# Latent attention: value products capped at four key tiles a step, a pair's last block in the step of tile 3, queries projected in two other steps

## The chip, the cores and the metric

The kernel runs on one core of a Trainium2 chip. The metric is the device time of one execution in microseconds (us). Three timed runs of the kernel before gave a median of 2326.03 us, with a lowest of 2324.08 and a highest of 2330.73. Engines are named as in the profile: PE is TensorE, DVE is VectorE, ACT is ScalarE, POOL is GpSimd, and SP is the engine whose queue issues most DMAs here.

## The reference

The computation has four layers over an input x of shape (2, 1024, 128), all in float32. Each layer is a normalization, an attention and a residual add, then a normalization, a feed-forward block and a residual add. The four attentions are called a, b, c and d after their tiles. Layer a shares one key and value head among 16 query heads and has no mask. Layer b is ordinary causal attention. Layer c is causal attention over a latent of 32 columns. Layer d is causal with biases. After a and b stands a quantized dense layer, after c and d a mixture of experts. The change touches layer c only:

```python
q_blhd = jnp.einsum('bld,dhk->blhk', x_bld, Wq)
latent_bll = jnp.einsum('bld,dc->blc', x_bld, Wkv_down)
k_blhd = jnp.einsum('blc,chk->blhk', latent_bll, Wk_up)
v_blhd = jnp.einsum('blc,chk->blhk', latent_bll, Wv_up)
attn = jnp.einsum('bqhd,bkhd->bhqk', q_blhd, k_blhd) / jnp.sqrt(jnp.asarray(HD, dtype=x_bld.dtype))
attn = jax.nn.softmax(jnp.where(mask, attn, neg_inf), axis=-1)
y_blhd = jnp.einsum('bhqk,bkhd->bqhd', attn, v_blhd)
return jnp.einsum('bqhd,hdo->bqo', y_blhd, Wout)
```

In the kernel the two up-projections are absorbed into the query weight and the output weight (`absorb`), so scores and value products of layer c work on the 32 latent columns themselves.

## The kernel before

**Units and steps.** A unit is one pair of heads of one batch of one layer: 4 layers x 2 batches x 8 pairs = 64 units, in that order. A unit of a causal layer has five steps, numbered i = 0 to 4, and a step takes the query tiles (128 rows each) listed in

```python
CAUSAL_STEPS = [[7], [6, 0], [5, 1], [4, 2], [3]]
```

so steps 0 to 3 each hold eight key tiles of scores for each head and step 4, that of tile 3, holds four. One loop runs over all steps of all units. The order is written out by hand (`tc.manual_schedule()`): every engine executes its instructions in the order in which this loop issues them.

**What one step issues, in this order.** (1) `transposes` of the step two places back: PE transposes probabilities (tiles `pp`, L788) and ACT copies them, or, for query blocks 2 and 3, DVE transposes them in 32 x 32 blocks into `slots` (L771). When a block of 256 query rows is complete, `blocks_moved` issues 16 DMAs on SP that reorder it into `prT` (L746). In front of this, `normalize` of the step one place back runs: DVE forms the reciprocal (L697) and POOL multiplies the probabilities (L701). (2) `add_products`: POOL adds finished outputs to x (L889). (3) `scores`: PE products `sc` (L634) and masks (L649), then DVE maxima `nmax` (L678). (4) `exponentials` on ACT (L689). The two score tiles in PSUM, one for each head, are reused by the next step, so its products wait for these exponentials. (5) `out_product` of what was finished in the step before: PE `po` (L866), and an ACT copy (L873). (6) `project`: a part of the next unit's projections, as many as the list `when` says for this step; in layer c a part is one half of the queries, one PE product of 128 x 512 in two passes (`pq`, L532) and one ACT copy (L540). (7) A part of the side work (normalizations and feed-forward blocks of the other batch). (8) `weigh_some`: value products `av` (L840) from a queue. (9) In step 4 the projection stands here, behind (8).

**The queue of value products.** The 1024 query rows of a unit are four blocks of 256 rows. They are accumulated in one PSUM tile, in the order of `BANKS`: block 3, then blocks 0 and 1 together, then block 2. A part of the queue is one key tile of one block. Block 3 has 8 parts, block 0 has 2, block 1 has 4 and block 2 has 6: 20 parts a unit. Block 3 and block 0 enter the queue in step 0 of the next unit, block 1 in step 1, block 2 in step 2. Blocks 2 and 3 come through the DMAs and enter two steps after their last transposes. The last part of a bank brings an ACT copy (L856), and the next step issues its `out_product`.

`weigh_some(4)` takes four parts and stops behind the last of a bank. If the end of a bank is among the next two parts, it goes on to that end. Counted out over steps 0 to 4, it issues 4, 4, 6, 6 and 0 parts: all of bank [0, 1] in step 2, all of block 2 in step 3, none in step 4.

**Around the layer.** The query weight of layer c is loaded by one DMA (`wq_c`, L1096) at the start of the last unit of layer b, behind the 16 DMAs of a block on SP. The projections of the first unit of layer c are issued in that same unit.

Of the kernel before, what the change touches and what calls it, by code (L numbers as in the profile page):

```python
# [36 lines left out]
def kernel(ctx: ExitStack, tc: tile.TileContext, a: dict, out: bass.AP):  # L37
# [30 lines left out]
    def load_attn(names):  # L68
        w = {}
        for key, src in names.items():  # L70
            ap = a[src]
            if key == "wo":
                t = wpool.tile([P, NPAIR, D], F32, tag="wo", name=f"wo_{src}")
                nc.sync.dma_start(out=t, in_=ap.rearrange("(c p) d -> p c d", p=P))
            elif key == "wk2":
                t = wpool.tile([D, 2, DH], F32, tag=key, name=f"{key}_{src}")
                for h in range(2):
                    nc.sync.dma_start(out=t[:, h, :], in_=ap)
            else:
                t = wpool.tile(list(ap.shape), F32, tag=key, name=f"{key}_{src}")  # L80
                nc.sync.dma_start(out=t, in_=ap)
            w[key] = t
        return w
# [177 lines left out]
    def moe_group(nm, b, g, last, xT, eng=nc.gpsimd, other=None):  # L261
# [139 lines left out]
    layers = [  # L401
        dict(nm="a", causal=False, kind="shared", ffn=dense_group, fnm="f"),
        dict(nm="b", causal=True, kind="full", ffn=dense_group, fnm="g"),
        dict(nm="c", causal=True, kind="latent", ffn=moe_group, fnm="m"),
        dict(nm="d", causal=True, kind="bias", ffn=moe_group, fnm="n"),
    ]
# [191 lines left out]
    def blocked(u, qb):  # L598

        if qb not in BLOCKED[layers[u[0]]["kind"]]:  # L600
            return 0
        nk = keys(u, qb * TPA + TPA - 1)
        return nk if layers[u[0]]["causal"] else nk - 1
# [4 lines left out]
    def step_of(u, qts):  # L608
        k = f"{tag_of(u)}_{qts[0]}"
        at = {}  # L610
        if len(qts) == 2:
            at = {qts[1]: 0, qts[0]: keys(u, qts[1]) * P}
        else:
            at = {qts[0]: QB - min(QB, keys(u, qts[0]) * P // 2)}
        pr = probp.tile([P, 2, S], F32, tag="pr", name=f"pr_{k}")
        tot = small.tile([P, 2, len(qts)], F32, tag="tot", name=f"tot_{k}")
        return dict(u=u, qts=qts, at=at, k=k, pr=pr, tot=tot)
# [66 lines left out]
    def exponentials(st, h, sc, nmax):  # L684

        u, tot = st["u"], st["tot"]
        for n, qt in enumerate(st["qts"]):
            c = slice(st["at"][qt], st["at"][qt] + keys(u, qt) * P)
            nc.scalar.activation(  # L689
                st["pr"][:, h, c], sc[:, c], AF.Exp, bias=nmax[:, n : n + 1],  # L690
                accum_out=tot[:, h, n : n + 1],
            )

    def normalize(st):
        u, pr = st["u"], st["pr"]
        rec = small.tile([P, 2, len(st["qts"])], F32, tag="rec", name=f"rec_{st['k']}")
        nc.vector.reciprocal(out=rec, in_=st["tot"])  # L697
        for h in range(2):
            for n, qt in enumerate(st["qts"]):
                c = slice(st["at"][qt], st["at"][qt] + keys(u, qt) * P)  # L700
                nc.gpsimd.tensor_scalar(  # L701
                    out=pr[:, h, c], in0=pr[:, h, c], scalar1=rec[:, h, n : n + 1], scalar2=1.0,
                    op0=ALU.mult, op1=ALU.mult,
                )
# [176 lines left out]
    def add_products():  # L881


        apply_coefficients()
        while adds:
            add_one(*adds.popleft())
# [47 lines left out]
    def some(queue, n):  # L934

        while n >= 1 and queue:
            try:
                next(queue[0])
                n -= 1
            except StopIteration:  # L940
                queue.popleft()
        return n
# [3 lines left out]
    def side_part():  # L946


        while side:
            try:  # L950
                said[0] = next(side[0])
                return
            except StopIteration:
                side.popleft()
        said[0] = None

    side, products, outs, waiting, complete, done = deque(), deque(), deque(), deque(), {}, {}
# [3 lines left out]
    def begin(u):  # L961
        for bank in banks(u):
            for qb in bank:
                late.append(dict(key=(u, qb), bank=bank, ready=None))

    def release():

        x = late.popleft()
        (u, qb), bank = x["key"], x["bank"]
        assert x["ready"] is not None  # L970
        nkt = keys(u, (qb + 1) * TPA - 1)
        products.extend(
            (u, qb, bank, kt, qb == bank[-1] and kt == nkt - 1) for kt in range(nkt)
        )

    def weigh_some(n):

        while n and products:
            part = products.popleft()
            weigh(*part)  # L980
            n -= 1
            if part[-1]:
                return
        if any(x[-1] for x in [*products][:2]):
            while not part[-1]:
                part = products.popleft()
                weigh(*part)
# [97 lines left out]
    for step, (n, u, qts, i, total) in enumerate([*steps, *[(None, None, None, 0, 1)] * 4]):  # L1085
        new = None
        if n is not None:
            if n != last:
                last = n
                some(coming, 9)  # L1090
                if n + 1 < len(units):
                    nu = units[n + 1]
                    if nu[:2] != u[:2]:
                        if nu[0] == 2 and 2 not in weights:
                            wq = wpool.tile([D, H * DH], F32, tag="wq", name="wq_c")
                            nc.sync.dma_start(out=wq, in_=c_wqk.rearrange("d p h c -> d (p h c)"))  # L1096
                            weights[2] = {"wq": wq}
                        elif nu[0] not in weights:
                            weights[nu[0]] = load_attn(w_names[nu[0]])
                        while nu[:2] not in xTs:  # L1100
                            side_part()
                    coming.append(project(nu))


                    if layers[nu[0]]["kind"] == "shared":
                        when = [0, 0, 1, 0, 1, 0, 0, 0]
                    elif layers[nu[0]]["kind"] == "latent":
                        when = [1, 1, 0, 0, 0]
                    elif total == NT:
                        when = [0, 1, 1, 0, 1, 1, 1, 1]  # L1110
                    else:
                        when = [1, 1, 2, 0, 2]
            new = step_of(u, qts)


        st = waiting.popleft() if len(waiting) == 2 or not new and waiting else None
        if st:
            if st["u"] not in begun:
                begun.add(st["u"])
                begin(st["u"])  # L1120
            for _ in transposes(st):
                if last_step:
                    normalize(last_step.pop())
            for qb in {qt // TPA for qt in st["qts"]}:
                if complete[st["u"], qb] == TPA:
                    x = next(x for x in late if x["key"] == (st["u"], qb))
                    x["ready"] = step + (2 if blocked(st["u"], qb) else 0)
        if last_step:
            normalize(last_step.pop())
        add_products()  # L1130
        if new and said[0] == "early":
            side_part()
            share -= 1
        if new:
            sc, nmaxs = scores(new)
            for h in range(2):
                exponentials(new, h, sc[h], nmaxs[h])
            last_step.append(new)
            waiting.append(new)
        while copies:  # L1140
            nc.scalar.copy(*copies.popleft())
        while outs:
            out_product(*outs.popleft())

        values = new and i >= (total - 2 if total == NT else total - 1)
        if new and coming and not values:
            some(coming, when[i])
        share = min(share + (1.8 if n is None else SIDE[u[0]]), 3.0)
        while share >= 1 and side:
            side_part()  # L1150
            share -= 1
            if said[0]:
                break


        while late and late[0]["ready"] is not None and late[0]["ready"] <= step:
            release()
        weigh_some(4)
        if values and coming:
            some(coming, when[i])  # L1160
    while products or late or outs or side:
# [67 lines left out]
```

## Time and profile before

| | value |
|---|---|
| median of the timed runs | 2326.03 us |
| profiled execution | 2320.46 us, of which the span from first to last instruction is 2318.7 us |
| mean granted clock of PE | 0.968 |
| busy share of the span | PE 91%, DVE 74%, ACT 63%, POOL 55% |
| scores of layer c on PE (`sc_c`) | from 1192.5 to 1678.2 us |
| first and last start of its value products (`av_c`) | 1226.6 and 1703.8 us |
| parts of projections of layer c (`pq_c`) | 32, in 64 passes, from 1167.1 to 1627.7 us |

The busy shares are means over stages that differ. Layers a, b and d keep PE almost without a gap. In layer c the products are short and PE waits more. The place of the layer is read from the first and last start of its tiles. The clock column is the share of full speed that PE was granted: where it says 0.50, a product takes about twice as long.

### The profile page before, as it was taken

To read this page: it belongs to the slowest core of one execution; us is meant where nothing else is said; L and a number is where in the kernel's file an instruction comes from. 1 tells how busy PE (TensorE), PEld (TensorE's weight loads), DVE (VectorE), ACT (ScalarE), POOL (GpSimd) and SP (SyncE) were. 2 spreads that over 40 slices of the span, in tenths; PEclk is the share of its full clock that TensorE was granted. 3 is DMA by queue.
4 is the path that set the end of the run, shared out by engine and by line. 5 is a ranking of instruction groups with operands and counts; after the bars stand their busy time and mean duration, and the time that the engine had idled before them with its cause. 6 is when DMAs were issued, how large, how long until landed. Compare 5 with 4: busy or idle time off the path is not lost.

```text
span 2318.7 us, 43436 instructions
## 1 busy us (share of the span) xinstructions
PE 2111.9 (91%) x14833; PEld 1234.0 (53%) x14833; DVE 1717.2 (74%) x2695; ACT 1450.9 (63%) x3276; POOL 1282.9 (55%) x1723
## 2 busy tenths in 40 slices
PE   6999999999999999999987888888889999999986
PEld 2454444444445666666654444444455666656653
DVE  5979999999986876678668867867666656766544
ACT  3667676667765666666655566665666557666552
POOL 3756666767764554464545645655554446544441
PEclk8999999999999999999998889999899999999997
DMA  5767676667776666666655555554665446646450
GB/s 126 164 150 168 162 165 162 146 144 165 167 195 147 160 155 158 163 157 154 147 122 132 128 128 128 136 120 101 159 160 137 118 115 158 159 118 146 109 135 9
DMA packets 147195, 328.84 MB, mean 142 GB/s; under 512 B 48800, under 2 KB 59296, under 8 KB 146976
## 3 DMA queue, kind: packets, MB, share of 16 engines
q1 hardware_dynamic: 146976, 326.06, 59.5%
q8 instruction: 120, 1.97, 0.4%
q14 instruction: 99, 0.81, 0.1%
HBM read 10.27 MB, written 2.10 MB: 5 GB/s over the span
## 4 chain that ended last, share of the span: by engine, by line
PE 53%; DVE 13%; SPq 13%; ACT 8%; DMA 6%; issue 4%; POOL 2%; DVEq 0%; ACTq 0%; POOLq 0%
SPq L746 13%; PE av_a L845 6%; PE sc_a L634 6%; PE av_d L845 5%; DMA prT<-slots 5%; PE sc_d L634 4%; DVE slots L771 4%; PE sc_b L634 4%; PE av_b L845 3%; ACT pr_c L689 3%; PE sc_c L634 2%; DVE nmax_d L678 2%; DVE nmax_a L678 2%; DVE nmax_c L678 2%; PE pp_d L788 2%
## 5 line engine op out<-in xcount | busy, mean ns | idle before, releaser
L689 ACT ACTIVATE pr_a<-sc_a,nmax_a 128x1024 f32<-128x1024 f32 x256 | 282.8, 1109 | 216.0 <-DVE nmax_a L678 215.2
L701 POOL TENSOR_SCALAR pr_a<-pr_a,rec_a 128x1024 f32<-128x1024 f32 x256 | 283.4, 1118 | 188.2 <-DVE rec_a L697 187.8
L701 POOL TENSOR_SCALAR pr_d<-pr_d,rec_d 128x1024 f32<-128x1024 f32 (+7 forms) x256 | 186.3, 745 | 269.0 <-DVE rec_d L697 268.7
L678 DVE TENSOR_REDUCE nmax_a<-sc_a 128x1 f32<-128x1024 f32 x256 | 298.8, 1206 | 35.9 <-PE sc_a L634 35.4
L701 POOL TENSOR_SCALAR pr_b<-pr_b,rec_b 128x1024 f32<-128x1024 f32 (+7 forms) x256 | 186.8, 747 | 219.9 <-DVE rec_b L697 219.4
L701 POOL TENSOR_SCALAR pr_c<-pr_c,rec_c 128x1024 f32<-128x1024 f32 (+7 forms) x256 | 186.9, 747 | 207.0 <-DVE rec_c L697 207.0
L678 DVE TENSOR_REDUCE nmax_d<-sc_d 128x1 f32<-128x1024 f32 (+7 forms) x256 | 177.2, 748 | 149.8 <-PE sc_d L640 149.8
L689 ACT ACTIVATE pr_c<-sc_c,nmax_c 128x1024 f32<-128x1024 f32 (+7 forms) x256 | 186.3, 738 | 152.3 <-DVE nmax_c L678 125.4
L771 DVE STREAM_TRANSPOSE slots<-pr_a 128x896 f32<-128x896 f32 x256 | 279.0, 1094 | 3.0 <-DMA prT<-slots 1.5
L689 ACT ACTIVATE pr_b<-sc_b,nmax_b 128x1024 f32<-128x1024 f32 (+7 forms) x256 | 186.3, 738 | 146.6 <-DVE nmax_b L678 121.9
L634 PE MATMUL sc_a<-k_a,q_a 64*128 64x512 f32 x512 | 265.7, 633 | 11.7 <-ACT pr_a L689 11.5
L689 ACT ACTIVATE pr_d<-sc_d,nmax_d 128x1024 f32<-128x1024 f32 (+7 forms) x256 | 186.4, 738 | 135.2 <-DVE nmax_d L678 131.8
L634 PE MATMUL sc_a<-k_a,qx_a 64*128 64x512 f32 x512 | 263.1, 635 | 4.1 <-DMA qx_a<-q_a 4.0
L678 DVE TENSOR_REDUCE nmax_b<-sc_b 128x1 f32<-128x1024 f32 (+7 forms) x256 | 176.7, 746 | 88.6 <-PE sc_b L640 88.6
L845 PE MATMUL av_a<-prT,v_a 128*64 128x256 f32 x1792 | 223.0, 388 | 18.3 <-DMA prT<-slots 17.5
L678 DVE TENSOR_REDUCE nmax_c<-sc_c 128x1 f32<-128x1024 f32 (+7 forms) x256 | 176.9, 748 | 84.5 <-PE sc_c L649 83.7
L845 PEld LDWEIGHTS av_a<-prT,v_a 128*64 128x64 f32 x1792 | 122.5, 137 | 133.5 <-issue 76.4
L634 PE MATMUL sc_d<-k_d,q_d 64*128 64x512 f32 (+3 forms) x416 | 159.9, 497 | 0.3 <-ACT pr_d L689 0.3
L634 PE MATMUL sc_b<-k_b,q_b 64*128 64x512 f32 (+3 forms) x416 | 158.9, 494 | 1.1 <-ACT pr_b L689 1.1
L634 PE MATMUL sc_d<-kx_d,qx_d 64*128 64x512 f32 (+3 forms) x416 | 154.2, 490 | 0.2
L634 PE MATMUL sc_b<-kx_b,qx_b 64*128 64x512 f32 (+3 forms) x416 | 153.4, 488 | 0.7 <-ACT pr_b L689 0.6
L771 DVE STREAM_TRANSPOSE slots<-pr_b 128x1024 f32<-128x1024 f32 (+3 forms) x128 | 130.5, 1025 | 9.4 <-DMA prT<-slots 8.6
(407 smaller groups left out, 4743.7 us busy)
## 6 DMA issues: line engine op xcount, KB each, us to landing
prT<-slots SPq DMA_DIRECT2D x768, 128.0 KB, 2.3
prT<-slots SPq DMA_DIRECT2D x832, 112.0 KB, 2.2
prT<-slots SPq DMA_DIRECT2D x768, 96.0 KB, 2.1
qx_a<-q_a SPq DMA_DIRECT2D x32, 256.0 KB, 3.5
qx_b<-q_b SPq DMA_DIRECT2D x32, 256.0 KB, 3.6
kx_b<-k_b SPq DMA_DIRECT2D x32, 256.0 KB, 3.4
qx_d<-q_d SPq DMA_DIRECT2D x32, 256.0 KB, 3.6
kx_d<-k_d SPq DMA_DIRECT2D x32, 256.0 KB, 3.5
```

Source lines behind the costliest of these rows:

```text
L634: yield nc.tensor.matmul(sc[h][:, at[qt] + k0 : at[qt] + k1], lhsT=q[r, qt * P : (qt + 1) * P], rhs=kk[r, k0:k1], start=True, stop=not dia ...
L678: nc.vector.tensor_reduce(out=nmax[:, n : n + 1], in_=sc[h][:, c], axis=AX.X, op=ALU.max, negate=True)
L689: nc.scalar.activation(st["pr"][:, h, c], sc[:, c], AF.Exp, bias=nmax[:, n : n + 1], accum_out=tot[:, h, n : n + 1],)
L701: nc.gpsimd.tensor_scalar(out=pr[:, h, c], in0=pr[:, h, c], scalar1=rec[:, h, n : n + 1], scalar2=1.0, op0=ALU.mult, op1=ALU.mult,)
L746: nc.sync.dma_start(out=o, in_=x)
L771: nc.vector.transpose(dst, src.rearrange("p (k r q) -> p k r q", r=4, q=32),)
L788: nc.tensor.transpose(pt[:, h, kt - k0, :], pr[:, h, c0 : c0 + P], ident)
L845: nc.tensor.matmul(shaped(av[ROWS[h], n], t0), lhsT=vs[u][:, kt, h, :], rhs=moving(h, kt, t0), start=(kt == 0), stop=(kt == nkt - 1),)
```

## The change

`weigh_some` gets a second argument, with which going on to the end of a bank is switched off. Where the head of the queue belongs to a latent unit, the loop asks for four parts a step, and for six in the last step of a unit. The list `when`, which places the two halves of a latent unit's queries, goes from steps 0 and 1 to steps 1 and 3.

```diff
-    def weigh_some(n):
+    def weigh_some(n, more=True):
...
-        if any(x[-1] for x in [*products][:2]):
+        if more and any(x[-1] for x in [*products][:2]):
             while not part[-1]:
                 part = products.popleft()
                 weigh(*part)
...
                     elif layers[nu[0]]["kind"] == "latent":
-                        when = [1, 1, 0, 0, 0]
+                        when = [0, 1, 0, 1, 0]
...
-        weigh_some(4)
+        if products and layers[products[0][0][0]]["kind"] == "latent":
+
+            weigh_some(6 if i == total - 1 else 4, False)
+        else:
+            weigh_some(4)
```

Counted out in the same way, the steps 0 to 4 now issue 4, 4, 4, 2 and 6 parts: two parts of bank [0, 1] go from step 2 to step 3, and all six of block 2 from step 3 to step 4. The out-products follow one step behind: that of bank [0, 1] goes from step 3 to step 4, that of block 2 from step 4 to step 0 of the next unit, and their additions to x on POOL go one step later too. No instruction is added or removed.

## The prediction

> **What bounds the kernel now.** The change lies between about 1160 and 1710 us, from the last unit of layer b to the first of layer d, so I read that stage alone. First the view of waits for PE there (who was waited for: total, times, longest):
>
> ```profile
> PE sc_c L634 <- ACT pr_c L689: 24.0, 47, 1.2
> PE pp_c L788 <- POOL pr_c L701: 19.1, 23, 2.7
> PE av_c L840 <- DMA prT<-slots: 9.3, 6, 2.2
> PE po_c L866 <- DMA wo_c<-c_wvo: 4.1, 1, 4.1
> PE pq_c L532 <- DMA wq_c<-c_wqk: 3.5, 1, 3.5
> ```
>
> PE waits here for three things that come back in every unit (exponentials before scores, POOL before the `pp` transposes, the DMA before value products) and for two that come once. Then the timeline of a unit without side work shows where they fall (start, duration, engine, line, tiles, count, gap and its releaser):
>
> ```profile
> 1427.72 0.70 PE L866 MATMUL po_c<-wo_c,attnT_c 128*128 128x128 f32 x4
> 1428.63 0.44 PE L788 MATMUL pp_c<-ident,pr_c 128*128 128x128 f32 x2 [0.21 <-POOL pr_c L701]
> 1429.96 0.66 PE L788 MATMUL pp_c<-ident,pr_c 128*128 128x128 f32 x4 [0.90 <-POOL pr_c L701]
> 1430.55 1.14 PE L634 MATMUL sc_c<-latT_c,q_c 32*128 32x512 f32 x8
> 1431.62 0.28 PE L649 MATMUL sc_c<-over_all,ident_b 128*128 128x128 bf16 x2
> 1431.74 1.08 PE L532 MATMUL pq_c<-xT,wq_c 128*128 128x512 f32 x2
> 1434.37 1.07 PE L840 MATMUL av_c<-prT,lat_c 128*32 128x256 f32 x16 [1.55 <-DMA prT<-slots]
> ```
>
> That is the end of step 4 and step 0 of the next unit. In step 4 PE has nothing between `po` and `pp`, and `pp` waits 1.1 us for POOL. In step 0 the products of block 3 wait for DMAs. Last, the view by windows of the same steps 3, 4 and 0, cut at the first score product (us, busy of each engine, granted PE clock):
>
> ```profile
> 1419.99:1425.67 5.68, 5.47 (x52) 3.07 (x52) 4.73 (x8) 3.86 (x12) 3.39 (x5) 1.00 0.32 74
> 1425.67:1430.55 4.88, 3.19 (x22) 1.85 (x21) 3.80 (x8) 4.29 (x13) 3.33 (x5) 1.00 0.92 208
> 1430.55:1436.40 5.85, 4.29 (x37) 2.04 (x37) 3.01 (x4) 3.86 (x8) 3.22 (x5) 1.00 0.79 183
> ```
>
> PE (first busy column) is busy 5.47 of 5.68 us in step 3, but 3.19 of 4.88 in step 4. Yet a step's floor is not PE's: it is the loop of scores, maxima, exponentials and the next scores, which the timeline gives as 5.6 us between the ends of exponentials in steps 1 to 3 of quiet units, and 3.2 in step 4. A second loop binds the unit: the block-3 transposes on DVE end in step 3 at 1422.48, 16 DMAs follow at 0.63 us each on SP, the products start at 1434.37 and the scores of step 1 at 1436.4. PE is the bound only in steps where its next scores start later than the exponentials allow. I call that lateness and read it for all 80 steps from their timelines (scores can start 0.14 us behind the first head's exponentials at best).
>
> **Part 1: the queries leave step 0; the border of b and c.** The first latent queries were issued in step 0 of b's last unit, in front of b's value products, and `wq_c` was just being loaded:
>
> ```profile
> 1163.36 0.24 PE L640 MATMUL sc_b<-over,unit 64*128 64x128 bf16 x2
> 1167.14 1.10 PE L532 MATMUL pq_c<-xT,wq_c 128*128 128x512 f32 x2 [3.54 <-DMA wq_c<-c_wqk]
> 1168.17 3.63 PE L845 MATMUL av_b<-prT,v_b 128*64 128x256 f32 x16
> 1171.73 1.09 PE L788 MATMUL pp_b<-ident,pr_b 128*128 128x128 f32 x8
> ```
>
> With the queries in steps 1 and 3 the b products come first. Their own 16 DMAs were issued by 1162.6 and the last landed at 1164.3, so they start there, after a wait of 0.7 us. In the next step the same 16 take 1.73 us, so they end at 1166.1; eight `pp` (their POOL input was done at 1161.7) end at 1167.1. Scores of step 1 then start near 1167.2 instead of 1172.75; the exponentials they need ended at 1166.2. That is 5.5 us earlier. `wq_c` lands at 1167.0, before the query product of step 1. The second query product (1.1 us) comes into step 3, but behind it stands step 0 of c's first unit, where b's products wait 2.9 us for DMAs that are set by an earlier transpose, so it is hidden. I take -5.3. The lower end is -2.4 (3.54 less 0.7, less 0.4 for a landing that is delayed): the clock behind the gap was half (3.63 us against 1.73), and may be half again.
>
> [...]
>
> ```profile
> 1386.70:1390.10 3.40, 2.54 (x17) 1.33 (x18) 2.44 (x4) 2.68 (x10) 1.16 (x2) 1.00 0.64 158
> 1390.10:1393.50 3.40, 3.40 (x33) 2.03 (x32) 3.40 (x5) 2.02 (x5) 1.53 (x3) 0.50 0.20 47
> ```
>
> PE was busy 2.54 of 3.40 us, its longest gap was 1.21, and the clock still fell to 0.50. By that row every thinned step can bring a half-speed stretch of 3.4 us, worth up to 1.7 us. But five such stretches begin behind a POOL wait in step 4 (1253.6, 1284.3, 1315.0, 1376.5, 1649.5), which the change fills. I take 0, with ends of -8 (five by 1.7) and +10 (six new ones).
>
> **Part 2: two parts leave step 2.** Six parts with two zero products took 1.49 us (1417.59 to 1419.08), and 24 passes without them 1.49; a part is four passes and 0.25 to 0.27 us. So step 2 loses 0.5 us. This counts where step 2 was late: by more than 0.5 in units 1, 2, 4, 5, 6, 10, 11, 13, 14 and 15, by 0.3 in unit 3, by nothing in 7, 8, 9 and 12. Unit 0 still works off b's queue.
>
> **Part 3: step 3.** It loses six parts (1.49) and the out-product of bank [0, 1] (1.11, row x8 at 1422.63), and gains two parts (0.5) and a query product (1.08): -1.0 us. It was late by that much only in units 4, 9, 10, 12, 13 and 14. On ACT the query copy (0.6) comes and the copy of the out-product (0.59) goes. The queue of SP and the DVE order are not touched in this step.
>
> **Part 4: step 4.** It gains six parts (1.49), and its out-product grows from two query tiles to four (0.70 to 1.11): +1.9 to 2.0 us in front of `pp`, and behind `pp` the scores of the next unit. The POOL wait covers 1.1 us in quiet units, 1.8 to 3.8 in units 1, 2, 3 and 14, about 0.3 to 0.9 in the others. So the scores of step 0 come 0.9 us later in quiet units. What is late next there is the DMA of step 0: its landing is set by step 3's transposes, PE's wait of 1.55 shrinks, and the scores of step 1 start as before. Without that cover (units 4 and 5) it costs 1.1 and 0.9, each less 0.45 from part 5. The ACT copy of block 2 (0.40) now queues in front of the `pp` copies and the exponentials of step 0; exponentials start at 1433.2 and these copies end near 1432.3: hidden. POOL loses an addition of 1.28 us here, behind which nothing urgent stood.
>
> **Part 5: step 0.** It loses a query product (1.08) and gains the out-product of block 2 (0.6): -0.45, worth something only where no DMA wait follows. The DMAs of block 2 (SP) write where the products of step 4 read, so they now wait for PE until about 1430.4 instead of 1425.2. But the DVE transposes in front of them end at 1431.0, and SP is busy with block 3 until 1432.6: nothing. Were SP held, 4.8 us without an issue lie before the next block's DMAs.
>
> **The sum.** Border -5.3. Unit 0: its step 3, late by 1.3, gains a query product, +1.0. Units 1 to 6: parts 2 and 3 give -3.8, parts 4 and 5 cost +1.1: -2.7. Units 7 to 9, bound by the DMA loop: 0. Units 10 to 13 carry the expert layer; there PE waits inside the side work for DVE, and what stands in front of that (`po`, `pq`) is hidden in every step, so only moved parts count: parts 2 and 3 give -4.5, part 4 costs 4 x 1.5 less some 3.0 of waits in step 4: -1.5. Unit 14: -1.3. Unit 15: its step 2 gives -0.5, its step 4 holds projections of d and has only 0.3 us of wait, +1.7, and as much as 0.3 of such waits falls due in d's first unit: +1.5. Together -8.3 us (border -5.3, +1.0, -2.7, -1.5, -1.3, +1.5). The side work of batch 0 also moves one step later, with the additions; its pieces keep their order and end in step 0 of unit 15, just in time; I count 0, with 3 us either way.
>
> The profiled span becomes 2318.7 - 8.3 = 2310.4 us (execution: 2312.2, with the same 1.8 around it). The median of the timed runs lies 5.6 above that execution; scaled, 2326.03 x 2310.4 / 2318.7 = **2317.7, so 2318 us**. Own range: 2311 to 2323, from the ends of the border and the noise of the side work.
>
> **Rivals.** (1) *Step 4 becomes the bound.* The pile-up of 2.0 us, less 1.1 of POOL wait, reaches the end in all 15 units and what steps 2 and 3 give up was covered by the exponentials: 15 x 0.9 = +13.5, border -5.3, together +8.2: 2334. For it: the exponentials are waited for 47 times. Against: the DMA wait of step 0. It decides once the distance from the scores of tile 3 to those of tile 7 grows by over 0.9 us while step 0 doesn't shrink. (2) *Only an exchange of waits.* The border's gain is taken back by the next DMA wait (2.9 us at c's first unit), the rest cancels: -1 to -3, so 2324. For it: quiet units are bound by the DMA loop. (3) *The clock gains.* A filled step 4 keeps full speed: another -8, so 2310.
>
> **How the numbers follow.** The forecast has 0.55, rival 1 0.22, rival 2 0.16, rival 3 0.07. About 0.3% (7 us) is what a measurement of this kernel can tell from no change. Faster by more than that, below 2319: rival 3 and two thirds of the forecast, 0.44. Within: the rest of the forecast and rival 2, 0.34. Slower: rival 1, 0.22. The range 2307 to 2332 leaves out about 0.1 at each end.
>
> **What would show it.** Right: no wait of `pq_c` for `wq_c`; scores at 1436.4 of the quiet unit unchanged against the start of its step 3; the `pp` wait for POOL well below 19.1 us. Wrong: quiet units longer than 26.3 us, more than 16% of the layer at half speed (mean clock 0.92), or `av_c` waiting on PSUM in step 4.

## The result and the profile after

The changed kernel takes 2333.01 us (median of 20 runs, 2324.92 to 2344.4), beside 2324.32 us for the kernel before (20 runs): a ratio of 1.0037, 95% interval [1.0025, 1.0049], or 8.7 us slower. The profiled execution took 2339.49 us (span 2337.8), in the upper part of those runs.

The view of waits for PE from 1160 to 1730 us, the changed kernel (who was waited for: total, times, longest):

```profile
PE sc_c L634 <- ACT pr_c L689: 30.0, 54, 1.7
PE cb_m L372 <- DVE sg_m L357: 10.5, 7, 1.7
PE pp_c L788 <- POOL pr_c L701: 9.3, 14, 1.2
PE av_c L840 <- DMA prT<-slots: 8.5, 6, 2.2
PE pp_c L788 <- ACT attnT_c L873: 2.3, 2, 1.4
PE gg_m L352 <- ACT q_c L540: 1.5, 1, 1.5
PE pt_d L174 <- POOL xn_d L157: 1.1, 1, 1.1
```

The wait for POOL halved (19.1 before) and that for `wq_c` (3.5) is gone, as foreseen. The wait for the exponentials grew from 24.0 to 30.0 us, and that of the second transposes for the copy of an out-product from 1.0 to 2.3. The wait of layer d's transposes for POOL is new. The expert layer's gate product now waits for the copy of the queries, 1.5 us; before, it waited 2.6 us for the copy of an out-product, so this wait is no loss.

The border of b and c in the timeline:

```profile
1163.44 1.95 PE L845 MATMUL av_b<-prT,v_b 128*64 128x256 f32 x16 [0.88 <-DMA prT<-slots]
1165.32 1.09 PE L788 MATMUL pp_b<-ident,pr_b 128*128 128x128 f32 x8
1166.35 0.59 PE L634 MATMUL sc_b<-k_b,q_b 64*128 64x384 f32 x1
...
1168.53 1.13 PE L532 MATMUL pq_c<-xT,wq_c 128*128 128x512 f32 x2
```

b's value products no longer stand behind the queries: they start 4.7 us earlier (1168.17 before), and the query product finds its weight there.

The quiet unit of the prediction, steps 4 and 0:

```profile
1419.83 2.08 PE L866 MATMUL po_c<-wo_c,attnT_c 128*128 128x128 f32 x8
1421.83 2.02 PE L840 MATMUL av_c<-prT,lat_c 128*32 128x256 f32 x24
1423.79 0.87 PE L788 MATMUL pp_c<-ident,pr_c 128*128 128x128 f32 x6
1424.59 1.14 PE L634 MATMUL sc_c<-latT_c,q_c 32*128 32x512 f32 x8
1425.66 0.28 PE L649 MATMUL sc_c<-over_all,ident_b 128*128 128x128 bf16 x2
1425.78 0.66 PE L866 MATMUL po_c<-wo_c,attnT_c 128*128 128x128 f32 x4
1427.52 1.07 PE L840 MATMUL av_c<-prT,lat_c 128*32 128x256 f32 x16 [1.08 <-DMA prT<-slots]
```

The same stretch by windows (us, busy of PE, PEld, DVE, ACT and POOL, granted clock, DMA share and rate): first step 3, then the end of step 3 with the beginning of 4, then the rest of step 4, then the whole of step 4 and step 0.

```profile
1411.89:1417.52 5.63, 4.64 (x30) 1.88 (x30) 4.68 (x8) 3.32 (x11) 3.39 (x5) 1.00 0.31 70
1416.00:1419.40 3.40, 1.99 (x14) 1.02 (x12) 2.54 (x5) 3.38 (x10) 1.15 (x3) 1.00 0.87 199
1419.50:1424.60 5.10, 5.10 (x44) 3.39 (x42) 3.26 (x6) 3.24 (x9) 4.58 (x7) 0.67 0.93 207
1417.52:1424.59 7.07, 6.43 (x49) 3.98 (x49) 4.38 (x8) 5.21 (x14) 4.95 (x7) 0.76 0.94 210
1424.59:1429.55 4.96, 3.88 (x39) 2.26 (x38) 2.36 (x2) 3.05 (x7) 0.35 (x1) 1.00 0.57 132
```

Step 4 takes 7.07 us (4.88 before), step 0 4.96 (5.85), step 3 5.63 (5.68): the three together are 1.3 us longer, not equal. Step 0 does give some back, for its DMA wait shrank as foreseen (1.55 to 1.08). But the pile-up in step 4 did not run at the price that I gave it. PE was busy only 1.99 of 3.40 us around the border of steps 3 and 4; then the clock fell, and `po` x8 with the six parts took 2.08 and 2.02 us where full speed gives 1.11 and 1.49, as in step 3 of the kernel before:

```profile
1422.63 1.11 PE L866 MATMUL po_c<-wo_c,attnT_c 128*128 128x128 f32 x8
1423.67 1.49 PE L840 MATMUL av_c<-prT,lat_c 128*32 128x256 f32 x24
```

The units in which the time went are read from the first exponential of each. A second profile of the kernel before was taken (span 2325.2); it has 174 us at half speed where the first has 147, and the last two columns compare the change with both. In this second one the three steps of the quiet unit take 16.95 us, against 16.41 in the first and 17.66 in the change.

| stretch | forecast | against the first profile | against the second |
|---|---|---|---|
| a and b up to the border | 0 | -1.0 | -1.3 |
| border of b and c | -5.3 | -4.5 | -4.4 |
| unit 0 | +1.0 | +0.8 | +0.5 |
| units 1 to 6 | -2.7 | -2.4 | -1.8 |
| units 7 to 9 | 0 | +3.6 | -1.0 |
| units 10 to 13 | -1.5 | **+9.7** | **+8.3** |
| units 14, 15 and d's first | +0.2 | **+8.2** | **+7.5** |
| the rest of d | 0 | +4.7 | +4.8 |
| sum | -8.3 | +19.1 | +12.6 |

The sums are those of single executions; the medians differ by 8.7. Most of the loss lies in units 10 to 15 of batch 1, where the expert layer runs beside the attention, and behind them.

### The profile page after: what moved, and what is told of

It reads as the page before. It is cut to its first block, busy times and chain, and to the rows that moved or that the text cites. A ratio compares the mean times of both kernels' runs of the same rounds, so it can differ in the third digit from the quotient of the medians.

```text
span 2337.8 us, 43429 instructions
## 1 busy us (share of the span) xinstructions
PE 2139.5 (92%) x14833; PEld 1244.7 (53%) x14833; DVE 1714.4 (73%) x2695; ACT 1453.2 (62%) x3276; POOL 1285.1 (55%) x1723
## 4 chain that ended last, share of the span: by engine, by line
PE 49%; SPq 16%; DVE 15%; ACT 8%; DMA 5%; issue 5%; POOL 3%; DVEq 0%; ACTq 0%; POOLq 0%
SPq L746 15%; PE sc_a L634 6%; PE av_a L845 5%; DMA prT<-slots 4%; DVE slots L771 4%; PE av_d L845 4%; PE sc_d L634 4%; PE sc_b L634 3%; PE av_b L845 3%; ACT pr_c L689 3%; PE sc_c L634 3%; DVE nmax_d L678 2%; DVE nmax_a L678 2%; DVE nmax_c L678 2%; PE av_c L840 2%
```

## The experiments

Times are medians; a ratio is to the kernel before, with its 95% interval. No kernel leaves work out; the filler products of some are read by nobody.

The expectations weigh the forecast's accounting against theories of the loss. *Pile-up*: the 2 us more in step 4 stand in front of the next unit's scores and no wait covers them. *Side work*: the normalizations and expert-layer pieces that follow a batch start once its last output has been added, and so one step later. *Clock*: steps with less work bring more stretches at half speed, such as the one behind the 1.99 busy us of 3.40 above. *PSUM* (from the runs within batch 1 on): out-products, query products and transposes take their PSUM tiles from one pool of three.

### The two halves of the change, and the side work

**Queries alone** (only the list `when` of the change).

> Kernel before with the list of the queries alone changed (steps 1 and 3 in place of 0 and 1). All three theories on the loss of the change leave this part out, so each expects the gain at the border of layers b and c alone: about 5 us less than before (ratio 0.998), no wait of pq_c for wq_c, and the rest of layer c as before. If it is not faster, moving the queries costs something that I have not seen, and the border's gain is taken back inside layer c.

Measured: 2325.86 us, 1.0020 [1.0011, 1.0028]: slower, although the border's gain is in it. Its waits show the price:

```profile
PE av_c L840 <- DMA prT<-slots: 19.9, 8, 3.6
```

That was 9.3 before. Without the query product PE reaches the value products of step 0 sooner and stands there, up to 3.6 us, before the DMAs have landed. No theory had foreseen this; all had expected 5 us less.

**Products alone** (the change without its line `when`).

> The changed order of value products alone, queries in steps 0 and 1 as before. Measured for the whole change is +8.7 us (ratio 1.0037); with a border gain of 5 us taken out, every theory expects about +13 us here (ratio 1.0055). They differ in where: pile-up theory: in step 4 of units 9 to 15; side-work theory: from unit 9 on, in the steps that hold the large pieces of the expert layer, whichever these are; clock theory: wherever the half-speed stretches lie, with some 45 us more at half speed over the span, each us at half speed worth up to half a us.

Measured: 2347.3 us, 1.0111 [1.0093, 1.013], 25.7 us slower where every theory had expected 13, and far worse than the whole change. A wait that was 1.0 us before has grown:

```profile
PE pp_c L788 <- ACT attnT_c L873: 12.3, 12, 2.3
```

`po`, `pq` and `pp` all take their PSUM tile from one pool of three (`ps_m`). With block 2's out-product and a query product both in step 0, the second transposes find none free until ACT has copied the out-product: twelve waits. With the queries moved away, two are left (2.3 us). That is 10 of the 17 us between the two kernels at most; the rest is not explained.

**Side work late**: the kernel before, but the side work behind layer c's batches enters one step later, as the later additions make it do in the change.

```diff
-            side.append(between(li, b))
+            (shifted if li == 2 else side).append(between(li, b))
```

> Kernel before, with value products and queries as they were; only the side work that follows a batch of layer c (expert layer and the start of layer d) enters one step later, as the change makes it do. Side-work theory: this alone brings most of the loss, +8 us or more (ratio 1.0035 or more). Pile-up theory: 0 within 2 us. Clock theory: 0 to +3 us.

Measured: 2335.38 us, 1.0057 [1.0041, 1.0072]. One step is enough: at the head of unit 15, what is left is forced in front of everything, and PE stands there (the line below). In the rest of layer d this kernel loses 4.8 us against the second profile of before, just as the change does.

```profile
PE pt_d L174 <- POOL xn_d L157: 5.3, 1, 5.3
```

**Batch 1 alone**: the change's order of products for batch 1 only, queries as before.

```diff
+        if products and layers[products[0][0][0]]["kind"] == "latent" and products[0][0][1] == 1:
```

> The changed order of value products for batch 1 of layer c alone (units 8 to 15); batch 0 and the queries as before, so that the expert layer of batch 0 starts in the step in which it did before. Pile-up theory: nearly all of the loss of the order stays, +10 us or more (ratio 1.004). Side-work theory: it is gone up to what the shifted side work of layer d brings, 0 to +3 us. Clock theory: about half of the loss of the order alone, +6 us.

Measured: 2337.34 us, 1.0060 [1.0041, 1.008]. The expert layer of batch 0 starts in its old step here, and only the start of layer d is still late. *Its products* below, with that caught up too, loses as much (1.0062), so this loss doesn't need the late side work.

### Catching up, and filling the thin step

**Caught up**: the change, and the late side work does two steps' share in its first step. **Caught up and filled**: the same with one product of 128 x 128 by 128 x 512 (1.1 us) in step 0, in front of block 3's products. **Queries filled**: this filler with the queries alone.

```diff
+            if layers[li]["kind"] == "latent" and qb == 3:
+                nc.tensor.matmul(
+                    pv_of[u].rearrange("p n q -> p (n q)"), lhsT=ident, rhs=m_gate[:, :QB],
+                    start=True, stop=True,
+                )
```

> The changed kernel, with the side work behind each batch of layer c doing two steps' worth in its first step (statistics of the normalization), so that every later piece stands in the step in which the kernel before had it. Side-work theory: the change loses by the late side work alone (measured by itself +13.8 us), so without it the gain at the border of b and c is left: 4 to 6 us below the kernel before (ratio 0.998), and pt_d no longer waits for POOL. Pile-up theory: the 2 us more in step 4 stay, so it remains slower than before by 5 us or more. Clock theory: it gains only as far as time at half speed falls; about +5 us stay.

> As the run caught_up, and in front of block 3's value products in step 0 of every latent unit one float32 product of 128 x 128 by 128 x 512 whose result is overwritten (1.1 us on PE at full speed, the size of the query product that the change took out of this place). Clock theory: step 0 stays busy while it waits for its DMAs, time at half speed falls by 15 us or more, and the kernel is as fast as caught_up or up to 5 us faster. Pile-up theory and side-work theory: the product is hidden in the DMA wait of quiet units and costs 1.1 us in some eight others: 0 to +9 us against caught_up.

> The kernel queries_only with the same extra product in step 0. Clock theory: queries_only lost its gain at the border because step 0 waits for DMAs with PE idle and goes on at half speed; with the product in its place it is 4 us or more faster than queries_only, at or below the kernel before. If the loss is only the query product now standing in step 3, late there by 1 us, the extra product doesn't help: the same as queries_only or up to 8 us slower.

Measured: caught up 2327.94 us, 1.0028 [1.0016, 1.004]; filled 2330.82, 1.0034 [1.0023, 1.0046]; queries filled 2322.28, 1.0004 [0.9993, 1.0014]. Catching up gives back 2 us of 8.7 by the ratios; the two intervals allow anything from none to 6, so lateness isn't the whole of the loss, and how much of it stays open. The filler makes the queries alone about 4 us faster (estimated from the two intervals, 0.5 to 7) although it adds 1.1 us of work to each unit. Steps 0 and 1 of unit 9 by windows, queries alone, then filled:

```profile
1452.34:1466.35 14.01, 9.46 (x71) 4.80 (x70) 7.94 (x23) 5.73 (x13) 4.84 (x6) 0.76 0.67 158
1455.03:1465.48 10.45, 7.67 (x71) 3.65 (x70) 7.94 (x23) 5.61 (x13) 4.83 (x6) 1.00 0.67 155
```

The same holds in units 7 to 10 together: steps 0 and 1 take 52.3 us with the queries alone, 23.9 of them at half speed, and 43.5 and 3.4 with the filler (41.8 and 0, 43.2 and 8.1 in the two profiles of before). So there the idle step 0 costs through the clock. The filler does nothing for the whole change, whose steps 0 and 1 there take 38.4 us, none at half speed.

### Which batch

**Border alone**: the kernel before, with the first latent unit's queries in steps 1 and 3. **First batch**: the change for units 0 to 6 only, its queries for batch 0 (so with the border). **Second batch, caught up**: the change from unit 7 on, without the border. **Before again**: nothing changed, for a second profile.

```diff
-                        when = [1, 1, 0, 0, 0]
+                        when = [0, 1, 0, 1, 0] if nu == units[32] else [1, 1, 0, 0, 0]
```

> Kernel before; only the queries of the first latent unit, issued in the last unit of layer b, go to steps 1 and 3. Forecast's first part: -4 to -5.5 us (ratio 0.998), and no wait of pq_c for wq_c. Clock theory: the same, since the queries that fill the DMA wait of step 0 inside layer c stay where they were. If the gain is taken back by the next DMA wait, it is 0.

> The change (order of value products and queries) in units 0 to 6 of layer c alone, with the border in it; batch 1 as before, side work in its old steps. Forecast's accounting: -1.5 us against border_only, about -6 us against before. Pile-up theory: in units without side work the POOL wait and the DMA wait cover step 4, 0 to +2 us against border_only. Clock theory: step 0 without its query product goes on at half speed in some units: +2 to +5 us against border_only.

> The change in units 7 to 15 alone (order of products from unit 7 on, queries of batch 1), with the late side work caught up; border and batch 0 as before. Caught_up measured +5.6 us against before and holds a border gain of 4.5. Pile-up theory: the loss sits here, +8 to +11 us (ratio 1.004), in step 4 of units 9 to 13, where it costs what it adds while the query product in step 3 takes back what the moved parts give. Forecast's accounting: about 0. Clock theory: a share by units, +4 to +6 us.

> The kernel before once more, for a second profile of it: how much of the differences between single profiles inside layer c is the clock's own scatter. If units 6 to 12 again have only 3 us at half speed, that is a property of the kernel before; if they have some 15 us, as the other kernels have, the one profile of before was a fortunate one, and up to 5 us of each difference in these units is scatter.

Measured: border 2318.49 us, 0.9982 [0.9973, 0.9991], 4.3 us faster than the 2322.79 beside it; first batch 2320.58, 0.9991 [0.9982, 1.0]; second batch 2337.14, 1.0071 [1.0057, 1.0084]; before again 2326.92 in one run. The border is worth what its step said. The order of products and queries gains nothing in batch 0 (2.1 us worse than the border alone, with intervals that overlap) and loses some 16 us (by the ratio, five runs) in batch 1. The second profile of before shows how far one kernel scatters: 27 us more at half speed and 6.5 us longer, 0.24 us for each. The border alone is the fastest kernel of this study, ahead of both.

### Within batch 1

**Its products**: the second batch, caught up, with the queries as before. **Its queries**: the kernel before with batch 1's queries in steps 1 and 3. **With the border**: second batch, caught up, and border. **One product in step 4**: the kernel before, with one filler of 1.1 us at the end of step 4 in the eight units of batch 1.

```diff
+        if n is not None and u[0] == 2 and u[1] == 1 and i == total - 1:
+            pf = ps_av.tile([P, 2, AB], F32, tag="av", name=f"pf_{n}")
+            nc.tensor.matmul(
+                pf.rearrange("p n q -> p (n q)"), lhsT=ident, rhs=m_gate[:, :QB],
+                start=True, stop=True,
+            )
```

> As second_caught_up (+14.3 us against before), but all queries in steps 0 and 1 as before: the order of products in units 7 to 15 alone. Pile-up theory (the 2 us more in step 4 are on the path, and the query product in step 3 takes back what the moved parts give): 3 to 6 us faster than second_caught_up. PSUM theory (three tiles in the pool of ps_m: the out-product of block 2 in step 0 beside a query product leaves none for the second transposes, which then wait for the ACT copy of the out-product): pp_c waits for ACT attnT_c by 5 us or more in all, and it is slower than second_caught_up, +17 us or more against before.

> Kernel before with the queries of batch 1 alone in steps 1 and 3. Theory that the query product in step 3 stands in front of the gate product and shifts the chain behind it: +3 to +6 us against before. Clock theory of step 0: about the same, +3 us, with longer waits of av_c for DMA in units 7 to 9 and half speed behind them. If neither holds, 0: then the loss of second_caught_up lies in the products alone.

> second_caught_up with the border of layers b and c changed too. If the parts simply add up: 14.3 - 4.3 = +10 us against before. Caught_up, which differs only in units 0 to 6, measured +5.6 with an interval of 2.8 either way; if this one is at +10, the rest of caught_up's difference is that batch 0's order helps once the border is changed, or scatter of the two; if it is at +4 or less, the parts don't add up, and the time in units 7 to 15 depends on where the clock's windows fall.

> The disputed cost by itself: kernel before, with one float32 product of 128 x 128 by 128 x 512 (1.1 us at full speed, result unused) at the end of step 4 in the eight units of batch 1, in the place where the change puts block 2's products; nothing else is moved. Forecast: hidden in the POOL wait in units 8 and 14, on the path by 0.2 to 0.8 us in the others, together +2 to +4 us. Pile-up theory: on the path nearly everywhere in the units with side work, +6 us or more. If it is at 0 or below, work in step 4 is free, or pays for itself by the clock.

Measured: products 2336.42 us, 1.0062 [1.0047, 1.0076]; queries 2327.13, 1.0024 [1.0011, 1.0037]; with the border 2328.76, 1.0032 [1.002, 1.0045]; one product in step 4 2320.95, 0.9999 [0.9989, 1.001]. Both halves lose, the products more. The queries lose where the queries alone did: steps 0 and 1 of units 7 to 10 take 52.2 us, 23.9 at half speed; step 3 grows too (table below). The parts barely add up: the second batch (7.1 thousandths) and the border (-1.8) would make 5.3, and 3.2 were measured, a difference about as large as its interval. And 1.1 us more of PE in step 4 costs nothing that can be measured, where the forecast's accounting had 2 to 4 us. A wait doesn't cover all of it: step 4 of units 9 to 13 grows by 2.1 to 2.7 us of the 5.5 added. Time at half speed fell from 161 to 148 us on average, so the clock may have paid for the rest.

### How much pile-up, and of what

**Sixteen thin products** and **two full ones**: as the last, with 2.0 us of products that use 32 columns (the lines below), or with two of the full product, 2.2 us. **Out-product late**: the kernel before, with block 2's out-product held from step 4 to step 0 in batch 1; no value product moves.

```diff
+            for j in range(16):
+                nc.tensor.matmul(
+                    pf[QUARTERS[j % 4], j // 4 % 2], lhsT=zeros, rhs=m_gate[:, :AB],
```

```diff
         while outs:
+            if n is not None and u[:2] == outs[0][0][:2] == (2, 1) and i == total - 1:
+                break
```

> The kernel before, with sixteen more products in step 4 of the eight units of batch 1 of layer c, each of a 128 x 32 tile of zeros with 128 x 256 numbers (32 passes of the form of a value product, some 2.0 us a step; their results are used by nothing). The pile-up theory (2 us of short products in step 4 stand in front of the next unit's scores and keep only a quarter of the array busy) expects +0.5% to +0.7% (12 to 16 us, the sum of step 4 over units 9 to 13 growing by 8 or more, as in second_products). The theory that the loss comes from the out-product of block 2 in step 0 and the PSUM tile it takes expects no more than +0.1%.

> The kernel before, with two more products of 128 x 128 by 128 x 512 in the same eight steps (2.2 us a step, of full rows and columns; their results are used by nothing). If it is the time in front of the next scores that costs, it is as slow as the kernel with sixteen thin products (+0.5% to +0.7%) or a little slower. If it is the little use of the array, and so the clock, it stays within 0.15% of the kernel before, with a clock of 0.965 or above. If neither costs, both kernels are within 0.1%.

> The kernel before, with only the out-product of block 2 (and so its addition) one step later, from step 4 to step 0 of the next unit, in units 8 to 14; no value product is moved. The PSUM theory (this product and the query product then take two of the three tiles in step 0, so that the second transposes of probabilities wait for the copy of the out-product) expects +0.3% to +0.6%, with a wait of those transposes for ACT's copy of 1 us in each of some seven steps, and step 0 of units 9 to 13 longer by 4 us or more. The pile-up theory expects no more than +0.1%, or a gain, since step 4 loses 0.7 us of PE work.

Measured, beside 2322.1 us: thin 2325.74, 1.0016 [1.0004, 1.0027]; two full 2325.1, 1.0016 [1.0004, 1.0029]; out-product late 2324.83, 1.0014 [1.0003, 1.0025]. Each costs 3 to 4 us (the intervals allow 1 to 7), a quarter to a half of what the theory behind it expected. Thin and full cost the same within their intervals, so nothing here speaks for the use of the array; what they share is the time that they take in front of the next scores. The late out-product had three waits for the copy (1.8 us), not seven. Units 9 to 13 by step (sums over five units, in us, each step from its first score product to the next step's):

| kernel | step 0 | 1 | 2 | 3 | 4 | sum |
|---|---|---|---|---|---|---|
| before, first profile | 32.6 | 26.7 | 41.1 | 40.4 | 22.8 | 163.6 |
| before, second profile | 31.7 | 27.1 | 42.8 | 42.6 | 22.2 | 166.4 |
| two full products in step 4 | 32.3 | 27.6 | 41.3 | 38.9 | 30.1 | 170.2 |
| sixteen thin ones | 30.3 | 27.6 | 41.3 | 38.9 | 31.0 | 169.1 |
| out-product late | 36.5 | 26.7 | 41.1 | 40.7 | 21.9 | 167.0 |
| batch 1's queries | 34.0 | 29.4 | 41.1 | 44.5 | 21.4 | 170.4 |
| batch 1's products | 36.4 | 26.7 | 44.2 | 36.4 | 29.6 | 173.3 |
| side work late | 34.9 | 26.7 | 35.9 | 43.7 | 28.8 | 170.0 |
| caught up | 32.2 | 28.2 | 43.7 | 39.7 | 29.7 | 173.6 |
| the change | 33.4 | 26.6 | 37.4 | 41.7 | 35.8 | 175.0 |

The row of the change can't be read step by step against before: its expert layer stands one step later, so that, for instance, 40 products of it (`po_m`) move from step 3 to step 4 of unit 13. *Side work late* shows that shift alone (step 4 28.8, no product moved), *caught up* the change without it (29.7).

The two prices stand side by side in the kernel with batch 1's products: its step 4 is as long as the pile-up makes it (29.6 beside 30.1 and 31.0), its step 0 as long as the late out-product makes it (36.4 beside 36.5). By the ratios the pile-up costs 3.7 us and the late out-product 3.3; if they add, that is 7.0 of the 14.4 us by which that kernel is slower.

The other half is not settled. The clock may hold part of it. The windows of units 9 to 13, batch 1's products, then sixteen thin ones, then the change, then the second profile of before:

```profile
1463.75:1637.09 173.34, 144.84 (x1122) 78.75 (x1121) 118.56 (x210) 101.49 (x255) 87.47 (x131) 0.92 0.47 108
```

```profile
1457.37:1626.49 169.12, 146.01 (x1282) 81.73 (x1281) 118.50 (x211) 101.47 (x255) 89.87 (x135) 0.96 0.49 113
```

```profile
1452.06:1627.02 174.96, 146.33 (x1121) 79.98 (x1120) 118.44 (x207) 101.42 (x255) 90.62 (x135) 0.91 0.47 109
```

```profile
1459.90:1626.31 166.41, 142.36 (x1122) 79.80 (x1121) 117.79 (x209) 100.85 (x254) 89.87 (x135) 0.92 0.50 115
```

The fillers, which leave steps 2 and 3 full, have 0.96 and the moved parts 0.92; but the kernel before has 0.97 in its first profile and 0.92 in its second, so single profiles don't tell them apart. Means of many runs do. Time at half speed, worked out from each run's granted clock as 2 x (1 - clock) x span, is on average 161 us before, 161 with the late out-product, 154 and 151 with the fillers, 183 with batch 1's products and 171 with the change. Over the change's 20 runs the span rises by 0.37 us for each us at half speed (correlation 0.85). At that slope the 22 us more of batch 1's products would be 8 us, which would fill the sum. But that is the steepest slope at hand but one: the runs of the kernel before beside the experiments give 0.08 to 0.29, and the six of batch 1's products 0.10, which makes 2 us. No run puts the clock back there alone, and the one filler given to the whole change lowered half speed from 166 to 153 us without a gain in time; so the other half stays open.

What a half-speed stretch costs within a step can be read where two kernels have work of the same form in it. Step 0 of unit 11, caught up, then the change:

```profile
1516.39:1525.67 9.28, 7.60 (x44) 3.83 (x44) 3.71 (x5) 4.93 (x9) 5.89 (x6) 0.82 0.61 145
1515.42:1523.07 7.65, 5.98 (x44) 2.85 (x43) 3.71 (x5) 4.77 (x9) 4.33 (x5) 1.00 0.65 156
```

One stretch of 3.4 us costs 1.6 us here. Step 2 of unit 10 takes 8.28 us in the kernel before without such a stretch and 8.28 in *out-product late* with one: there it costs nothing, perhaps because that step waits for the side work anyway, which isn't shown.

## Why the prediction was wrong

2318 was forecast, with a range of 2307 to 2332; 2333.01 was measured, on the other side of the kernel before.

- **The border** (-5.3) was right in mechanism and nearly in size: -4.5 in the trace, -4.3 as a kernel of its own. The wait of b's products was 0.88 us (0.7 taken), and their 16 products took 1.95 (1.73).
- **Unit 0** (+1.0) and **units 1 to 6** (-2.7) agree with the trace (+0.8 and -2.4), but the gain of units 1 to 6 doesn't show in medians, where the first batch is no faster than the border alone.
- **Units 7 to 9** (0): between -1.0 and +3.6, since the kernel before itself differs by 4.6 us there between its two profiles. The sign given for "wrong", quiet units longer than 26.3 us, tells nothing: unit 8 took 27.5, but 28.6 in the second profile of before. Nor does the sign of 16% at half speed: the change spends 24% of the layer there, from its first to its last score product, the kernel before 16% and 21%.
- **Units 10 to 13** (-1.5, measured +9.7 and +8.3): here the prediction failed. *Caught up*, where the side work stands as before, shows which terms (us over the four units):

| term | forecast | measured | read from |
|---|---|---|---|
| part 4: step 4 | +3.0 | +3.5 | 22.6 against 19.1, at full speed (unit 11 from *its products*) |
| parts 2 and 3: steps 2 and 3 | -4.5 | -2.3 | steps with the same clock on both sides (one from *its products*) |
| the clock | 0 | +5.5 and +4.1 | what is left of +6.7 and +5.3 against the two profiles |

  So part 4 was nearly right; two full fillers lengthen step 4 by 3.3 there. Parts 2 and 3 were taken at twice their worth, and the clock, put at nothing, was the larger miss: *caught up* has 27.3 us at half speed in these units, the two profiles of before 6.8 and 13.7. Three stretches at 1.6 us, in step 0 of units 11 and 13 and step 4 of unit 11, make about what is left. These are single profiles; the medians can't be split in this way. In the change itself step 4 grew by 10.2 us, but *side work late*, where no product moves, has 4.9 of that too.
- **"What stands in front of that (`po`, `pq`) is hidden in every step"**: not so for an out-product in step 0 beside a query product. It costs 3.3 us by itself (0.7 to 5.8), and step 0 of unit 11 takes 8.60 us there at full speed instead of 7.65. But in the change the query product leaves that step, which takes 7.65 us as before.
- **The clock at 0**, with an end of +10: over all runs half speed rose by 10 us on average, which at slopes of 0.08 to 0.37 is 1 to 4 us. I had weighed the five thin stretches that the change fills, and not those which it makes at the border of steps 3 and 4, by taking step 3's products away: these two steps of units 5 to 8 have 20.5 us at half speed, and 0.3 and 2.6 in the profiles of before. The window from 1416.00 was busy for 1.99 of 3.40 us, and half speed followed: a mean clock of 0.67 from 1419.50 to 1424.60.
- **Unit 15 and the side work** ("just in time", 0 with 3 either way): units 14, 15 and d's first lost 7.5 us against +0.2, the rest of d 4.8. In the profile of *caught up* these are 2.2 and -1.8, and *side work late* has the same 4.8 in the rest of d, so the profiles put most of this on the late side work. By the medians catching up gives back 2 us, 6 at the most. The change's profiled run is 6.5 us above its median, so its profile may show more of this than a usual run has; the size stays open.
- **PSUM** was not priced at all: `po`, `pq` and `pp` share three tiles, and that is one reason why the products can't be moved without the queries; the queries without the products fail for another, the idle step 0. The change as it was drawn has 2.3 us of such waits instead of 12.3.

In all, the change loses some 13 us behind the border. The runs show that most of it is lost in batch 1, and they price a pile-up of this size at 3.7 us (1 to 7); late side work (0 to 6) and the clock (1 to 4) are estimates, and the sum isn't closed.

Rival 1 came near the measured number, 2334, by luck: it let all 15 units pay 0.9 us. Step 4 does grow by more than 0.9 us, but batch 0 loses little, and what batch 1 loses is only in part the pile-up.

## What to carry to other kernels

A step that waits can take in some work, but less than its wait suggests: measure it with fillers of one and two sizes before moving real work into it. When comparing step by step, check that the same work stands in each step, and at the same clock; two profiles of one kernel can differ by more than the effect. Before moving a product, list what shares its PSUM pool and what will be copied in front of what, and price the step that is thinned as well as the one that is filled. A part of a change that pays by itself (here one line for one unit, 4.3 us) is worth more than the whole around it.

## What was not expected of the hardware

In this case's traces half speed came behind windows in which PE was busy, above all behind those with little work in them. In the profiler's clock records every stretch at one speed, but the last of each trace, is a multiple of 3.41 us. For each window of that length at full speed in all twenty traces (12544 of them), I summed over the products the moving columns, times rows used / 128, times columns used / 128, where 128 of each is the largest product in these traces. Below 1071 the next window was at half speed in 263 of 263 cases, from 1071 to 1608 in 287 of 369, from 1608 to 2110 in 29 of 535, and above that in 0 of 11377. Only 12 of these 579 falls came behind a window less than 5% busy. In the profiles of before and after alone the same counts are 29 of 29, 30 of 40, 1 of 58 and 0 of 1126, and 1 of the 60 falls came behind a window less than 5% busy.

Other measures separate these windows worse. With the best single limit, 78 windows stand on the wrong side of it for this sum, 172 when columns used are left out, 369 when rows used are left out, and 398 for plain busy time (11, 16, 39 and 35 of the 1253 windows of the two profiles). Full speed came back behind 1 of 308 windows at half speed with a sum below 1385, and behind 416 of 416 above 1839. In this sum a score or value product of layer c, with 32 rows or 32 columns, counts a quarter; 386 of the 579 falls lie between 1192 and 1700 us, where 2390 of the windows are. The window of the change that begins at 1416.13, with scores of 32 rows, has a sum of 1035 and is one of the falls.

These are counts, with limits set after the fact. That the sum is the cause was not shown: no run changes it alone, and the thin and the full fillers add the same to it, 2048 a step.
